# Cross-attention on one core: an output bias on one partition, context rows loaded a round later, and two sets of context squares put behind fetches in SyncE's queue

## The chip, the cores and the metric

The kernel runs on one core of a Trainium2 chip. A core has five engines that run side by side: TensorE (PE, matrix multiplication), VectorE (DVE), ScalarE (ACT), GpSimd (POOL) and SyncE (SP). Here nearly every DMA is issued by SyncE, whose instructions run strictly in order. The metric is the device time of one launch in microseconds, the median of several runs.

## The reference

Sixty-four independent items b, each with text rows x[b] (256 x 512) and context rows c[b] (256 x 384), all in float32:

```
Q = layer_norm(x @ W_text + b_text) * g1 + beta1       # 256 x 512
V = c @ W_audio + b_audio
K = layer_norm(V) * g2 + beta2                         # 256 x 512
alpha = softmax(Q @ K.T / sqrt(512))                   # 256 x 256
out = layer_norm((alpha @ V) @ W_out + b_out + x) * g_out + beta_out
```

## The kernel before

Everything is tiled to 128 partitions: an item has two row tiles of x and two of c. The value path is folded: since the rows of alpha sum to one, (alpha @ V) @ W_out is (alpha @ c) @ (W_audio @ W_out) plus a row vector b_audio @ W_out + b_out. The folded weights are built once (`fold_multiply`, tile `wao`). The row vector is built in two steps: `bias_parts` sums, over four groups of rows, W_out's rows scaled by b_audio into `part` (128 x 512), and `fold_bias` multiplies `part` by a matrix of ones, which sums over the partitions and puts the same row on each of the 128 partitions; VectorE then adds `bo_sb`, the output bias broadcast to all partitions by a 256 KB DMA, while it takes the sum out of the accumulator (`bao`).

The matrix multiplications need operands with the contracted dimension on partitions. The kernel gets such transposes by way of DMA. `squares` issues four DMAs (lines 84 to 88) that lay a matrix out in blocks of 32 x 32, one DMA for each group of 32 partitions, and VectorE transposes within the blocks. For the inputs this is `load_c` (tile `cq`, 4 x 96 KB) and `load_x` (tile `xq`, 4 x 128 KB). For computed Q and K rows it is a round trip through device memory: `store` writes the normalised rows (`qr`, `kr`; 512 KB) to a scratch tensor (`qd`, `kd`) in one DMA, `fetch` reads it back as squares (`qq`, `kq`; 4 x 128 KB), `turn` transposes them into `qT` or `kT`, and `affine` lets ScalarE apply the scale and the shift. The exponentials take the same way (`ed`, `eq`). A fetch waits on SyncE until the store has landed, and all that is written behind it in the program waits too.

The schedule is written out by hand: each engine's instructions run in the order of the program. A prologue does the projections of items 0 and 1 and the foldings; then a loop of 62 rounds runs. Round b computes the scores and the softmax of item b, the query and key projections of item b + 2, the context product (`Attention.context`, L587) of item b - 1 and its output product, and finishes item b - 2. The squares of item b + 4 are loaded in round b. Plain rows are loaded too: `load_x_rows` for the residual and `load_c_rows` for the context product, each of which has three buffers. In round b the row loads are those of x[b] and of c[b + 1]. Both come in SyncE's order behind the squares and the fetch of the exponentials. The accumulators of the projections are six banks of pool `p_pj`.

The end of the prologue is where the change lies. In the program's order SyncE has there: store of k[0], the five small loads of the column vectors, fetch of k[0], store of q[0], `load_c(2)`, fetch of q[0], `load_x(2)`, store of k[1], the broadcast of the output bias, `load_c(3)`, fetch of k[1], `load_x(3)`, store of q[1], fetch of q[1]. Behind this begins round 0, and round 1 begins with the scores of item 1, which need `qT` and `kT` of item 1.

Of the kernel before, what the change touches and what calls it, by code (L numbers as in the profile page):

```python
# [9 lines left out]
F32 = mybir.dt.float32  # L10
AF = mybir.ActivationFunctionType
ALU = mybir.AluOpType
# [3 lines left out]
P = 128  # L16
# [6 lines left out]
def kernel(  # L23
# [41 lines left out]
    nc = tc.nc  # L65
# [3 lines left out]
    H = w_text.shape[1]  # L69
# [4 lines left out]
    const = ctx.enter_context(tc.tile_pool(name="const", bufs=1))  # L74
# [9 lines left out]
    def squares(dst, src):  # L84

        v = src.rearrange("(b j) (q f) -> q j b f", j=SQ, q=NQ)
        for q in range(NQ):
            nc.sync.dma_start(dst[q * SQ : (q + 1) * SQ], v[q])  # L88
# [7 lines left out]
    def load_c(b):  # L96
        cq = blk.tile([P, S // SQ, DA // NQ], F32, tag="cq", name=f"cq_{b}")
        squares(cq, c[b])
        blocks[b] = [cq]

    def load_x(b):
        xq = blk.tile([P, L // SQ, D // NQ], F32, tag="xq", name=f"xq_{b}")
        squares(xq, x[b])
        blocks[b].append(xq)
# [5 lines left out]
    def load_x_rows(b):  # L110
        x_rows[b] = xin.tile([P, LT, D], F32, tag="x", name=f"x_{b}")
        nc.sync.dma_start(x_rows[b], x[b].rearrange("(t p) d -> p t d", p=P))

    def load_c_rows(b):
        c_rows[b] = cin.tile([P, ST, DA], F32, tag="c", name=f"c_{b}")
        nc.sync.dma_start(c_rows[b], c[b].rearrange("(t p) d -> p t d", p=P))
# [16 lines left out]
    def row(v, name):  # L133
        t = const.tile([P, H], F32, tag=name, name=name)
        nc.sync.dma_start(t, v.rearrange("(o h) -> o h", o=1).broadcast_to([P, H]))
        return t
# [8 lines left out]
    x_rows, c_rows = {0: x_0}, {0: c_0}  # L145
# [21 lines left out]
    load_x(1)  # L167
    columns = const.tile([P, 5, HC], F32, tag="columns", name="columns")

    def load_vectors():  # L170
        for n, v in enumerate((g1, beta1, g2, beta2, b_audio)):
            nc.sync.dma_start(
                vectors[n * HC : (n + 1) * HC].rearrange("k (q i) -> k q i", q=NQ),
                v.rearrange("(q k i) -> k q i", q=NQ, i=SQ),
            )
# [21 lines left out]
    class RowTurn:  # L197


        def __init__(self, rows_sb, chunks, name):  # L200
            self.rows, self.chunks = rows_sb, chunks
            tag = "yr" if chunks == DC else "kT"
            self.ar = work.tile([P, 2, chunks, P], F32, tag=tag, name=f"{name}r")
            self.T = work.tile([P, chunks, 2 * P], F32, tag=name, name=f"{name}_0")
# [25 lines left out]
    def bias_parts():  # L230

        part = work.tile([P, D], F32, tag="e", name="part")
        nc.vector.tensor_scalar(part, wo_sb[:, 0, :], bac_sb[:, 0:1], None, ALU.mult)
        for k in range(1, HC):
            nc.vector.scalar_tensor_tensor(
                part, wo_sb[:, k, :], bac_sb[:, k : k + 1], part, ALU.mult, ALU.add
            )
        return part

    wao_sb = const.tile([P, AC, D], F32, tag="wao", name="wao")  # L240
# [17 lines left out]
    def fold_bias(part):  # L258

        ps = p_pj.tile([P, D], F32, tag="pj", name="ps_bao")  # L260
        nc.tensor.matmul(ps, lhsT=ones, rhs=part, start=True, stop=True)
        bao = const.tile([P, D], F32, tag="bao", name="bao")
        nc.vector.tensor_tensor(bao, ps, bo_sb, ALU.add)
        return bao

    def moments(mv, src, t):
# [242 lines left out]
    class Attention:  # L509
        def __init__(self, b):  # L510
            self.b, self.qT, self.kT = b, q.pop(b).T, k.pop(b).T
            self.c_sb, self.summed = c_rows[b], ()

        def scores(self, end=False):
            if end:
# [62 lines left out]
        def context(self):  # L578

            self.zT = work.tile([P, AC, L], F32, tag="zT", name="zT")  # L580
            self.ps_z = []
            for lo in range(0, AC, 2):
                n = min(2, AC - lo)
                ps = p_at.tile([P, 2, L], F32, tag="at", name="ps_z")
                for j in range(n):
                    for s in range(ST):
                        nc.tensor.matmul(  # L587
                            ps[:, j, :],
                            lhsT=self.c_sb[:, s, bass.ts(lo + j, P)],
                            rhs=self.eT[:, s, :],  # L590
                            start=(s == 0),
                            stop=(s == ST - 1),
                        )
                nc.scalar.copy(self.zT[:, lo : lo + n, :], ps[:, :n, :])
# [163 lines left out]
    def turn_next(b):  # L758
        xT[b] = turn_x(b)
        xs[b] = sum_x(xT.pop(b))  # L760
        cT[b] = turn_c(b)
        cs[b] = sum_c(cT.pop(b))
# [7 lines left out]
    q, k, xT, cT = {}, {}, {}, {}  # L770
# [41 lines left out]
    k[0].normalise()  # L812
    k[0].store()
    load_vectors()
    k[0].fetch()
    q[0].evict(0)
# [3 lines left out]
    centre(bt_row, mean_bt, 1)  # L820
    q[0].normalise()
    q[0].store()
    load_c(2)
    q[0].fetch()
    load_x(2)
    xT[1] = turn_x(1)
    k[1].products(6)
# [16 lines left out]
        nc.vector.tensor_scalar(v, v, scale, None, ALU.mult)  # L844
    k[1].normalise()
    k[1].store()
    bo_sb = row(b_out, "bo")
    load_c(3)
    k[1].fetch()
    load_x(3)  # L850
    fold_evict(0)
    fold_evict(1)
    k[0].turn()
    k[0].affine(g2_sb, be2_sb)
    part = bias_parts()
    q[1] = Blocks("q", 1, xs.pop(1), wt_blocks, bt_sb)
    q[1].products(1, 2, 6, 5)
# [15 lines left out]
    fold_multiply(2)  # L873
    fold_evict(2)
    bao_sb = fold_bias(part)
    wao_blocks = weights_of_three(wao_sb, "waosum")
    q[1].normalise()
# [4 lines left out]
    for b in range(B - 2):  # L882
        three = b + 3 < B
        at = Attention(b)
        at.scores()
        if done:
            done.o.leave(3, 4)
            done.o.leave(7)
            done.add_x()
        if three and b:  # L890
            turn_next(b + 3)
        if last:
            last.turn_e()
        at.maxima()
        at.exponentials()
        if not b:
            k[1].turn()
        q2 = q[b + 2] = Blocks("q", b + 2, xs.pop(b + 2), wt_blocks, bt_sb)
        q2.products(*((1, 6) if b else (1, 2, 6)))
        q2.leave(1)  # L900
        q2.leave(6)
        at.reciprocals()
        at.divide_e()
        if not b:
            k[1].affine(g2_sb, be2_sb)
        if b:
            q[b + 1].fetch()
            k[b + 1].fetch()
        at.store_e()
        if b + 4 < B:  # L910
            load_c(b + 4)
        if not b:
            at.fetch_e()
        if b + 4 < B:
            load_x(b + 4)
        if b:
            at.fetch_e()
            load_x_rows(b)
        if not three:
            load_x_rows(b + 1)  # L920
        load_c_rows(b + 1)
        if b == 1:
            go_sb = row(g_out, "go")
            beo_sb = row(beta_out, "beo")
        if done:
            done.statistics()
        q2.products(*((2, 5) if b else (5,)))
        q2.leave(2, 5)
        q2.products(3, 4)
        q2.leave(3, 4)  # L930
        q2.products(7)
        q2.leave(7)
        q2.square()
        q2.scales()
        q[b + 1].turn()
        if not b:
            turn_next(3)
        if done:
            done.shift(0)
            done.shift(1)  # L940
        if last:
            last.context()
        q[b + 1].affine(g1_sb, be1_sb)
        if b:
            k[b + 1].turn()
            k[b + 1].affine(g2_sb, be2_sb)
        if done:
            done.settle(0)
            done.settle(1)
            done.store()  # L950
        q2.normalise()
        q2.store()
        if last:
            last.start_products()
        k2 = k[b + 2] = Blocks("k", b + 2, cs.pop(b + 2), wa_blocks, ba_sb)
        k2.products(1, 6)
        k2.leave(1)
        k2.leave(6)
        k2.products(2, 5)
        k2.leave(2, 5)  # L960
        k2.products(3, 4)
        k2.leave(3, 4)
        k2.products(7)
        k2.leave(7)
        k2.square()
        k2.scales()
        k2.normalise()
        k2.store()
        if last:
            last.o.products(1, 6)  # L970
            last.o.leave(1)
            last.o.leave(6)
            last.o.products(2, 5)
            last.o.leave(2, 5)
            last.o.products(3, 4)
            last.o.products(7)
        done, last = last, at
# [112 lines left out]
```

## Time and profile before

| what | value |
|---|---|
| median of 3 runs | 1416.42 us (1416.02 to 1416.92) |
| the profiled execution | 1416.99 us, span 1415.2 us |
| PE busy | 1404.5 us, 99% |
| DVE busy | 1229.0 us, 87% |
| ACT busy | 935.1 us, 66% |
| POOL busy | 870.6 us, 62% |
| DMA | 322.58 MB, mean 228 GB/s |
| mean granted PE clock | 0.999 |

Times inside the profile are counted from the start of the span. The span is the profiled execution without what lies around it (1.8 us). "SPq" is SyncE's queue: its rows show how long the issue of a DMA took, and a separate view gives the time from issue to landing. PE and PEld are the matrix multiplications and the loads of their stationary operands. L numbers are lines of the kernel.

### The profile page before, as it was taken

The page shows a single profiled execution, that of the slowest core. Times are in us where ns is not written, and L with a number is a line of the kernel's source. Part 1 is how long each engine was busy: PE and PEld are TensorE (multiplying, and loading weights), DVE is VectorE, ACT ScalarE, POOL GpSimd, SP SyncE. Part 2 cuts the span into 40 slices and gives each one's busy share as a digit, 9 for nine tenths or more (in the row PEclk, how much of TensorE's full clock was granted, in tenths as well). Part 3 has the DMA queues.
Part 4 walks back from the last instruction along what each step waited for, and adds up shares of the span by engine and source line. Part 5 has one row for each costly group of instructions (what it writes and reads, how often), then busy time and mean ns, then how long its engine had stood idle before and what let it go on. Part 6 is the DMA issues. An engine that isn't in the chain of part 4 may idle for free.

```text
span 1415.2 us, 22762 instructions
## 1 busy us (share of the span) xinstructions
PE 1404.5 (99%) x6437; PEld 1219.7 (86%) x6437; DVE 1229.0 (87%) x1757; ACT 935.1 (66%) x2298; POOL 870.6 (62%) x1294
## 2 busy tenths in 40 slices
PE   9999999999999999999999999999999999999998
PEld 5788888888888888888888888888888888888885
DVE  5789888988988988988889889889888898898887
ACT  4667676676676676766766766767667667667663
POOL 5557656656666666566566666665665665666645
PEclk9999999999999999999999999999999999999999
DMA  7898887887888787887887887877888788788864
GB/s 198 212 249 245 243 238 220 240 241 221 234 232 229 232 228 236 234 226 237 229 233 232 220 241 233 227 238 228 226 242 239 221 236 239 222 235 226 229 199 125
DMA packets 450579, 322.58 MB, mean 228 GB/s; under 512 B 154900, under 2 KB 382996, under 8 KB 450452
## 3 DMA queue, kind: packets, MB, share of 16 engines
q1 hardware_dynamic: 450356, 320.98, 80.0%
q8 instruction: 52, 0.85, 0.3%
q14 instruction: 75, 0.61, 0.1%
q10 hardware_dynamic: 96, 0.13, 0.0%
HBM read 204.09 MB, written 116.92 MB: 227 GB/s over the span
## 4 chain that ended last, share of the span: by engine, by line
PE 94%; DMA 3%; DVE 1%; POOL 1%; SPq 1%; ACT 0%; issue 0%; DVEq 0%; ACTq 0%
PE ps_q L482 26%; PE ps_k L482 20%; PE ps_y L482 20%; PE ps_sc L521 15%; PE ps_z L587 12%; DMA qd<-qr 1%; PE ps_y L634 1%; DMA ba<-in_L_xattn_b_audio_dram 1%; DMA qq<-qd 0%; DMA xq<-in_x_dram 0%; DMA bt<-in_L_xattn_b_text_dram 0%; SPq L88 0%; DMA c<-in_ctx_dram 0%; DVE qr L494 0%; DMA kd<-kr 0%
## 5 line engine op out<-in xcount | busy, mean ns | idle before, releaser
L494 DVE TENSOR_TENSOR qr<-ps_q,qr 128x512 f32<-128x512 f32 x252 | 174.3, 692 | 88.3 <-PE ps_q L482 85.3
L521 PE MATMUL ps_sc<-kT,qT 128*128 128x256 f32 x1024 | 231.7, 379 | 1.1 <-ACT qT L453 1.1
L348 POOL TENSOR_SCALAR ve<-var 128x2 f32<-128x2 f32 x126 | 43.1, 342 | 290.3 <-ACT junk L387 290.1
L521 PEld LDWEIGHTS ps_sc<-kT,qT 128*128 128x128 f32 x1024 | 194.2, 190 | 28.8 <-ACT qT L453 2.1
L538 ACT ACTIVATE e<-ps_sc,nmx 128x256 f32<-128x256 f32 x128 | 59.4, 469 | 228.7 <-DVE nmx L531 228.7
L603 POOL TENSOR_TENSOR yr<-yr,x 128x512 f32<-128x512 f32 x124 | 155.6, 1277 | 70.2 <-DVE yr L494 70.2
L482 PE MATMUL ps_q<-wtsum,xsum 128*128 128x256 f32 x756 | 193.8, 379 | 0.2 <-POOL xsum L312 0.2
L494 DVE TENSOR_TENSOR kr<-ps_k,kr 128x512 f32<-128x512 f32 x252 | 174.3, 692 | 22.1 <-DVE kr L494 0.5
L494 DVE TENSOR_TENSOR yr<-ps_y,yr 128x512 f32<-128x512 f32 x248 | 171.5, 692 | 21.8 <-DVE yr L494 0.5
L482 PE MATMUL ps_k<-wa,cT 128*128 128x256 f32 x630 | 177.1, 379 | 0.0
L587 PE MATMUL ps_z<-eT,c 128*128 128x256 f32 x768 | 176.2, 379 | 0.0
L482 PE MATMUL ps_y<-wao,zT 128*128 128x256 f32 x620 | 174.1, 379 | 0.0
L350 POOL TENSOR_TENSOR rstd<-ve,nhalf 128x2 f32<-128x2 f32 x192 | 157.1, 818 | 16.0
L587 PEld LDWEIGHTS ps_z<-eT,c 128*128 128x128 f32 x768 | 145.9, 190 | 20.3 <-issue 0.5
L482 PEld LDWEIGHTS ps_q<-wtsum,xsum 128*128 128x128 f32 x756 | 143.6, 190 | 20.0 <-POOL xsum L312 0.6
L453 ACT ACTIVATE qT<-qT,columns 128x256 f32<-128x256 f32 x256 | 132.9, 591 | 8.0 <-DVE qT L91 8.0
L482 PEld LDWEIGHTS ps_k<-wa,cT 128*128 128x128 f32 x630 | 119.6, 190 | 16.2
L453 ACT ACTIVATE kT<-kT,columns 128x256 f32<-128x256 f32 x256 | 132.0, 586 | 1.4 <-DVE kT L446 1.0
L415 ACT ACTIVATE kr<-kr,rstd 128x512 f32<-128x512 f32 x126 | 84.0, 714 | 72.3 <-POOL rstd L350 72.3
L482 PEld LDWEIGHTS ps_y<-wao,zT 128*128 128x128 f32 x620 | 117.7, 190 | 16.0
L387 ACT ACTIVATE junk<-kr 128x512 f32<-128x512 f32 x126 | 79.4, 630 | 77.5 <-DVE kr L494 73.1
L482 PE MATMUL ps_q<-wt,xT 128*128 128x256 f32 x504 | 129.1, 379 | 0.0
(159 smaller groups left out, 2973.0 us busy)
## 6 DMA issues: line engine op xcount, KB each, us to landing
kd<-kr SPq DMA_DIRECT2D x64, 512.0 KB, 3.1
kq<-kd SPq DMA_DIRECT2D x256, 128.0 KB, 3.4
qd<-qr SPq DMA_DIRECT2D x64, 512.0 KB, 4.8
qq<-qd SPq DMA_DIRECT2D x256, 128.0 KB, 3.3
xq<-in_x_dram SPq DMA_DIRECT2D x252, 128.0 KB, 2.8
x<-in_x_dram SPq DMA_DIRECT2D x63, 512.0 KB, 4.2
out_dram<-yr SPq DMA_DIRECT2D x62, 512.0 KB, 4.8
cq<-in_ctx_dram SPq DMA_DIRECT2D x252, 96.0 KB, 2.4
```

Source lines behind the costliest of these rows:

```text
L348: nc.gpsimd.tensor_scalar(ve, var, EPS, None, ALU.add)
L350: nc.gpsimd.tensor_tensor(r, ve, nhalf[:, :n], ALU.pow)
L387: nc.scalar.activation(junk, self.rows[:, t, :], AF.Square, scale=1.0 / math.sqrt(H), accum_out=self.var[:, t : t + 1],)
L415: nc.scalar.mul(row, row, self.r[t])
L453: nc.scalar.activation(self.T[:, k, :], self.T[:, k, :], AF.Identity, bias=bet[:, k : k + 1], scale=gam[:, k : k + 1],)
L482: nc.tensor.matmul(place, lhsT=side, rhs=w, start=(i == 0), stop=(i == len(pairs) - 1))
L494: add = lambda o, i0, i1: nc.vector.tensor_tensor(o, i0, i1, ALU.add)
L521: nc.tensor.matmul(self.sc[:, t, :], lhsT=self.qT[:, k, bass.ts(t, P)], rhs=self.kT[:, k, :], start=(k == 0), stop=(k == HC - 1),)
L538: nc.scalar.activation(self.e[:, t, :], self.sc[:, t, :], AF.Exp, bias=self.nmx[:, t : t + 1], accum_out=self.den[:, t : t + 1],)
L587: nc.tensor.matmul(ps[:, j, :], lhsT=self.c_sb[:, s, bass.ts(lo + j, P)], rhs=self.eT[:, s, :], start=(s == 0), stop=(s == ST - 1),)
L603: nc.gpsimd.tensor_tensor(self.y[:, t, :], self.y[:, t, :], x_rows[self.b][:, t, :], ALU.add)
L634: nc.tensor.matmul(ps, lhsT=self.zT[:, k, bass.ts(t, P)], rhs=wao_sb[:, k, :], start=(k == 0), stop=(k == AC - 1),)
```

## The change

The output bias is now loaded onto one partition (2 KB), as the first of the small loads in `load_vectors`, and VectorE adds it to partition 0 of `part` before the multiplication by ones, which then distributes it; the eviction into `bao` is a plain copy. From round 1 on, round b loads the context rows of item b instead of b + 1; round 0 loads none, and the last round of the loop, number 61, loads those of items 61 and 62. `Attention` looks its context rows up when it uses them. In the prologue the fetch of q[0] comes ahead of `load_c(2)`, and the fetch of k[1] ahead of `load_c(3)`.

```
+    bo_sb = const.tile([1, H], F32, tag="bo", name="bo")
     def load_vectors():
+        nc.sync.dma_start(bo_sb, b_out.rearrange("(o h) -> o h", o=1))
         for n, v in enumerate((g1, beta1, g2, beta2, b_audio)):
...
     def bias_parts():
...
+        nc.vector.tensor_tensor(part[:1], part[:1], bo_sb, ALU.add)
         return part
...
     def fold_bias(part):
...
-        nc.vector.tensor_tensor(bao, ps, bo_sb, ALU.add)
+        nc.vector.tensor_copy(bao, ps)
...
     class Attention:
         def __init__(self, b):
-            self.c_sb, self.summed = c_rows[b], ()
+            self.summed = ()
...
         def context(self):
-                            lhsT=self.c_sb[:, s, bass.ts(lo + j, P)],
+                            lhsT=c_rows[self.b][:, s, bass.ts(lo + j, P)],
...
     q[0].store()
+    q[0].fetch()
     load_c(2)
-    q[0].fetch()
     load_x(2)
...
     k[1].store()
-    bo_sb = row(b_out, "bo")
+    k[1].fetch()
     load_c(3)
-    k[1].fetch()
     load_x(3)
...
         if b:
             at.fetch_e()
             load_x_rows(b)
+            load_c_rows(b)
         if not three:
             load_x_rows(b + 1)
-        load_c_rows(b + 1)
+            load_c_rows(b + 1)
```

More of the change, by code (lines that the diff above doesn't have):

```diff
@@ L168 @@
     columns = const.tile([P, 5, HC], F32, tag="columns", name="columns")
+    bo_sb = const.tile([1, H], F32, tag="bo", name="bo")
     def load_vectors():
+        nc.sync.dma_start(bo_sb, b_out.rearrange("(o h) -> o h", o=1))
         for n, v in enumerate((g1, beta1, g2, beta2, b_audio)):
@@ L237, in bias_parts @@
             )
+        nc.vector.tensor_tensor(part[:1], part[:1], bo_sb, ALU.add)
         return part
@@ L262, in fold_bias @@
         bao = const.tile([P, D], F32, tag="bao", name="bao")
-        nc.vector.tensor_tensor(bao, ps, bo_sb, ALU.add)
+        nc.vector.tensor_copy(bao, ps)
         return bao
@@ L511, in __init__ @@
             self.b, self.qT, self.kT = b, q.pop(b).T, k.pop(b).T
-            self.c_sb, self.summed = c_rows[b], ()
+            self.summed = ()
         def scores(self, end=False):
@@ L588, in context @@
                             ps[:, j, :],
-                            lhsT=self.c_sb[:, s, bass.ts(lo + j, P)],
+                            lhsT=c_rows[self.b][:, s, bass.ts(lo + j, P)],
                             rhs=self.eT[:, s, :],
@@ L822 @@
     q[0].store()
+    q[0].fetch()
     load_c(2)
-    q[0].fetch()
     load_x(2)
@@ L846 @@
     k[1].store()
-    bo_sb = row(b_out, "bo")
+    k[1].fetch()
     load_c(3)
-    k[1].fetch()
     load_x(3)
@@ L918 @@
             load_x_rows(b)
+            load_c_rows(b)
         if not three:
             load_x_rows(b + 1)
-        load_c_rows(b + 1)
+            load_c_rows(b + 1)
         if b == 1:
```

## The prediction

> **What bounds the kernel now.** I read the chain that ended last first, since it names the engine that sets the end.
>
> ```profile
> PE 94%; DMA 3%; DVE 1%; POOL 1%; SPq 1%; ACT 0%; issue 0%; DVEq 0%; ACTq 0%
> ```
>
> TensorE (PE) carries the span. So a change can only act by making or closing a gap in PE's work, and the next view is everything that PE ever waited for. It has five rows, 3.6 us in all; this is the only one that lies beside the changed lines.
>
> ```profile
> PE ps_sc L521 <- ACT qT L453: 1.1, 1, 1.1
> ```
>
> It is the scores of round 1, and in the timeline of PE every later matmul of the main loop follows without idle time: a round is 21.58 us of matmuls (60.17 to 81.75 and on). Whatever delays or hastens that one instruction at 60.17 us moves the whole rest, one for one. The chain in order of time, cut to the first 66 us, tells what it waits for: the second queries' rows are stored (`qd<-qr`), fetched back as squares (`qq<-qd`), transposed, scaled, multiplied.
>
> ```profile
> 31.59 4.86 DMA qd<-qr
> ...
> 37.85 3.42 DMA qq<-qd
> ...
> 49.58 3.60 DMA qd<-qr
> ...
> 54.59 3.52 DMA qq<-qd
> ...
> 59.52 0.61 ACT qT L453
> 60.17 3.90 PE ps_sc L521 x16
> ```
>
> All these transfers are issued by one in-order queue, SyncE's (SP), so its timeline is the view that the change is read in. Columns: start, time, line, transfer, count.
>
> ```profile
> 31.59 0.40 SPq L425 DMA_DIRECT2D qd<-qr  x1
> 32.04 3.20 SPq L88 DMA_DIRECT2D cq<-in_ctx_dram  x4
> 36.51 1.79 SPq L88 DMA_DIRECT2D qq<-qd  x4
> 38.35 1.96 SPq L88 DMA_DIRECT2D xq<-in_x_dram  x4
> 40.42 0.39 SPq L425 DMA_DIRECT2D kd<-kr  x1
> 40.85 0.47 SPq L135 DMA_DIRECT2D bo<-in_L_xattn_b_out_dram  x1
> 41.36 2.62 SPq L88 DMA_DIRECT2D cq<-in_ctx_dram  x4
> 44.78 1.79 SPq L88 DMA_DIRECT2D kq<-kd  x4
> 46.63 1.92 SPq L88 DMA_DIRECT2D xq<-in_x_dram  x4
> 49.58 0.38 SPq L425 DMA_DIRECT2D qd<-qr  x1
> ```
>
> A fetch cannot be issued before its store has landed. Now each store is followed by work that fills that wait: context 2's squares (32.04 to 35.24) in the wait for `qd`, and the bias and context 3's squares (40.85 to 43.98) in the wait for `kd`. SP stands still for only 1.27 us (35.24 to 36.51) and 0.80 us (43.98 to 44.78). The store of q[1] at 49.58 starts when its rows are ready (ScalarE's `qr` ends at 49.56); SP had been free since 48.55.
>
> **The change in SP's queue.** It takes the fillers out of the two waits and puts them behind the fetches, in front of the next store.
>
> First wait. The store of q[0] stays at 31.59: the bias row's new issue (one, about 0.4 us by its neighbours, the loads of `vectors`) goes where SP sat from 29.26 to 29.71 waiting for k[0]'s store, so it costs 0 to 0.1 us. Does q[0]'s store land sooner without four transfers behind it? Three rows say that a store's landing depends on what is ahead: `kd` at 26.83 with an idle queue ahead took 2.81 us; `kd` at 40.42, straight behind four x squares, took 4.3; and the median `kd`, which has fetches right behind it, takes 3.1. Here the four `kq` fetches (29.71 to 31.50) are still ahead. I keep 4.86 us, hence the fetch at 36.51 as before; the low end is 3.6 (`qd` at 49.58), which gives 1.26 us back.
>
> Then SP issues `qq` until 38.30, `cq` of context 2 (four issues; 1.93 us, as the four x squares behind a fetch take 1.92 to 1.96; the high end is 3.20, the row of the same tile directly behind a store) until 40.3, and `xq` until 42.3. So k[1]'s store, whose rows are ready at 37.85, goes out at 42.3 instead of 40.42: 1.9 us late.
>
> Second wait. Straight behind x squares the landing is 4.3 us as now (low end 2.8): 46.6. Fetch `kq` 46.65 to 48.45, `cq` of context 3 to 50.4, `xq` to 52.4. The bias broadcast's 0.47 us is gone, but it lay in the wait and saves nothing there. The store of q[1] therefore goes out at 52.45 instead of 49.58, now bound by SP and not by its rows. Before, SP had been free for 1.0 us ahead of it and it landed in 3.60; now it follows the x squares directly, so I take 4.3: landed at 56.75 instead of 53.18. That is 3.55 us late; fetch, transpose and scaling keep their times, so PE's scores start at 63.7 instead of 60.17 and PE's gap grows from 1.1 to 4.6 us. **Sum of this part: +3.5 us.**
>
> The sum of issue times is not the only way to see this: from the start of `qq` at 36.51 to the landing of `kd` is 8.2 us now, with `qq`, `xq` and `kd` to move; four squares of context 2 between them add their 1.9 us, 10.1 us; the same pattern follows once more from `kq`. 36.45 + 2 x 10.1 gives 56.65. Both ways agree within 0.1 us.
>
> **What else it touches, costed at nothing.** PE's work between 44 and 59 us: any slip there is swallowed by the 4.6 us gap, as long as it is smaller. x squares of 2 now land near 45.4 (last issue 41.8 + 3.6) and the transpose that needs them starts at 46.24: 0.8 us left. `kq` of k[1] lands 1.9 us later, so VectorE's transpose at 49.91 goes to 51.8, and the five evictions of q[2] queued behind it end near 56.9 instead of 55.06; the accumulators that PE needs again from 57 us are the first ones emptied, by 54.4, and VectorE is free before the transpose of q[1], its next job, at 61.8. ScalarE's `e` and its store likewise stand before that.
>
> The bias: one 2 KB load and one VectorE add on one partition, queued between `part` (ends 39.28) and the transpose of q[0] at 41.39, in 2.12 us of idle time. Its nearest rows are 444 ns (L233) and 752 ns (L235); it fits, and would cost up to 0.75 us only if `qq` landed over a microsecond sooner. The eviction at L263 (0.65 us) becomes a copy of the same size; its reader is a round away.
>
> Context rows a round later: one issue and 384 KB leave round 0, and every round b then loads context b where it loaded b + 1. In the round at 643 us the load goes out at 658.03, and the next round's context matmuls, which now read it, start at 674.3: 16.3 us against a median landing of 4.8. Only the last main round issues one row load more (about 0.45 us at 1367.8), in front of SP's 2.8 us of idle time before 1371.53; its reader starts at 1380.49, so 7.9 us are left after a landing of 4.8. If either cover were gone, the shortfall would go straight to PE.
>
> **A gap of 4.6 us and PE's clock.** At the end of the trace PE's last matmul ends at 1408.35 and the windows show the granted clock (the third column from the right) holding for 4.1 us and then halved:
>
> ```profile
> 1408.40:1412.50 4.10, 0.00 (x0) 0.00 (x0) 3.83 (x9) 0.00 (x0) 2.12 (x3) 1.00 0.33 123
> 1412.60:1415.20 2.60, 0.00 (x0) 0.00 (x0) 0.00 (x0) 0.00 (x0) 0.00 (x0) 0.50 0.51 177
> ```
>
> So idle time of 4.2 us did bring it down, and 4.6 us may or may not. Its price is bounded by the cold start: there the first 12 matmuls of L195 took 2.93 us, where the same shape at L224 goes 6 in 0.82; that and the stretch behind it lost about 1.4 to 2.6 us. I take nothing for the likeliest case and keep 2.6 for the range.
>
> [...]
>
> **The rivals.** (1) The clock falls in the gap: +3.5 plus 1.4 to 2.6, 1421.3 to 1422.5. For it: the end of this trace; against: a gap barely longer than the time it held. (2) The landings are shorter: with fewer transfers in flight the three stores land in about 4.2, 3.8 and 3.8 us, and 0.7 + 0.5 + 0.5 come off: about +1.8, 1418.2. For it: q[1]'s own 3.60; against: the 4.3 behind x squares. (3) Not slower at all: stores land as on an idle queue. With 3.6, 2.8 and 2.8 us the sum is 3.55 - 1.26 - 1.5 - 1.5 = -0.7, PE's gap falls to 0.4, and at most the whole 1.1 us of waiting can go: 1415.3 to 1416.4. It decides where the three landings together are below 9.9 us (13.46 in my sum). Against it: x squares are directly ahead of two of the three stores.
>
> **How the numbers follow.** The profiled execution took 1416.99 us (its span of 1415.2 and 1.8 around it); with 3.5 that is 1420.5. The median of the runs, 1416.42, is 0.57 lower: 1419.9. What a measurement can tell from no change is about 0.2%, 2.8 us, that is 1419.25. The forecast (+2.3 to +4.6, the upper end from slower issues of the context squares) has 0.62, of which 0.5 lies over the bound and 0.12 under it; rival 1 has 0.20, rival 2 0.12, rival 3 0.06. Slower: 0.5 + 0.2 = 0.70; same: 0.12 + 0.12 + 0.04 = 0.28; faster 0.02, for a cause that I do not see, since PE has only 3.6 us of waits to give back. The range leaves out rival 3, part of rival 2, and what exceeds rival 1: 1417.6 to 1423.0.
>
> **What would show it.** In the profile after: the wait of `ps_sc` L521 for `qT` near 4.6 us instead of 1.1; SP waiting over 4 us for `qd` and for `kd` where it now waits 1.3 and 0.8; k[1]'s store near 42.3 and q[1]'s near 52.4 with no wait for `qr`; no PE wait at L587 for context rows; the rounds still 21.58 us. Wrong if q[0]'s store lands before 35.5, if q[1]'s store still waits for its rows, if a granted clock of 0.5 stands in the windows after 60 us, or if PE waits for `c`.

## The result and the profile after

The changed kernel is slower by 0.17%: ratio 1.0017, 95% interval 1.0011 to 1.0023; medians 1418.31 us against 1415.9 us, 22 runs each. The difference of 2.4 us lies in the predicted range, clear of no change, and inside the 0.2% below which the prediction counted a change as none. The profiled execution took 1417.74 us, its span is 1416.0.

The split of the chain that ended last is unchanged; TensorE (PE) still carries it:

```profile
PE 94%; DMA 3%; SPq 1%; DVE 1%; POOL 1%; issue 0%; ACT 0%; DVEq 0%; ACTq 0%; POOLq 0%
```

What PE waited for in the whole span (engine, line, what for: us in total, times, longest). The wait before round 1's scores has grown from 1.1 us, and among the five rows there is none at L592, the context product that reads the rows loaded later:

```profile
PE ps_sc L526 <- ACT qT L458: 3.0, 1, 3.0
```

SyncE's queue in the same stretch as before (start, us, line, transfer):

```profile
30.55 0.40 SPq L430 DMA_DIRECT2D qd<-qr  x1
35.59 1.82 SPq L88 DMA_DIRECT2D qq<-qd  x4
37.45 1.93 SPq L88 DMA_DIRECT2D cq<-in_ctx_dram  x4
39.42 1.93 SPq L88 DMA_DIRECT2D xq<-in_x_dram  x4
41.46 0.39 SPq L430 DMA_DIRECT2D kd<-kr  x1
45.14 1.79 SPq L88 DMA_DIRECT2D kq<-kd  x4
46.98 1.93 SPq L88 DMA_DIRECT2D cq<-in_ctx_dram  x4
48.97 1.92 SPq L88 DMA_DIRECT2D xq<-in_x_dram  x4
51.38 0.38 SPq L430 DMA_DIRECT2D qd<-qr  x1
54.86 1.79 SPq L88 DMA_DIRECT2D qq<-qd  x4
```

This execution runs about 1.04 us ahead at the store of q[0] (30.55 against 31.59), so rows are to be read as distances from it. Then SyncE (SP) stands still in both waits, which its own waits say:

```profile
SPq L88 <- DMA qd<-qr: 4.6, 1, 4.6
SPq L88 <- DMA kd<-kr: 3.2, 1, 3.2
```

Before, the same two rows were 1.2 and 0.7 us, and there was one of 0.9 us, in which the store of q[1] waited for its rows (`qr`). That one is gone: the rows are ready at 48.42 us, 3 us ahead of the store, which is now late by the queue. The chain of the same stretch:

```profile
30.55 5.02 DMA qd<-qr
...
41.46 3.66 DMA kd<-kr
...
50.95 0.42 issue
51.38 3.41 DMA qd<-qr
...
56.20 2.63 DMA qq<-qd
...
60.89 3.91 PE ps_sc L526 x16
```

From the store of q[0] to that of q[1] it is 20.83 us, where it was 17.99: 2.84 us more. From there to the scores it is 9.51 us, where it was 10.59: 1.08 us less. The difference of the two, 1.8 us, is about what PE's wait has grown by.

### The profile page after: what moved, and what is told of

Its sections match the earlier page's. It is cut to its first block, busy times and chain, and to the rows that moved or that the text cites. A ratio compares the mean times of both kernels' runs of the same rounds, so it can differ in the third digit from the quotient of the medians.

```text
span 1416.0 us, 22763 instructions
## 1 busy us (share of the span) xinstructions
PE 1403.7 (99%) x6437; PEld 1219.5 (86%) x6437; DVE 1230.8 (87%) x1758; ACT 937.5 (66%) x2298; POOL 871.7 (62%) x1294
## 4 chain that ended last, share of the span: by engine, by line
PE 94%; DMA 3%; SPq 1%; DVE 1%; POOL 1%; issue 0%; ACT 0%; DVEq 0%; ACTq 0%; POOLq 0%
PE ps_q L487 26%; PE ps_k L487 20%; PE ps_y L487 20%; PE ps_sc L526 15%; PE ps_z L592 12%; SPq L88 1%; DMA qd<-qr 1%; PE ps_y L639 1%; DMA wo<-in_L_xattn_W_out_dram 1%; DMA kd<-kr 0%; DMA x<-in_x_dram 0%; DMA wt<-in_L_xattn_W_text_dram 0%; DMA c<-in_ctx_dram 0%; DVE yr L499 0%; DMA qq<-qd 0%
## 5 line engine op out<-in xcount | busy, mean ns | idle before, releaser
L592 PE MATMUL ps_z<-eT,c 128*128 128x256 f32 x768 | 176.2, 379 | 0.0
L592 PEld LDWEIGHTS ps_z<-eT,c 128*128 128x128 f32 x768 | 145.9, 190 | 20.3 <-issue 0.5
```

The costliest lines, as they stand in the source:

```text
L592: nc.tensor.matmul(ps[:, j, :], lhsT=c_rows[self.b][:, s, bass.ts(lo + j, P)], rhs=self.eT[:, s, :], start=(s == 0), stop=(s == ST - 1),)
```

## The experiments

Ratios are against the kernel before on the same chip, with their 95% intervals.

### The order alone, and the rest alone

With both fetches put back into the changed kernel:

```
     q[0].store()
-    q[0].fetch()
     load_c(2)
+    q[0].fetch()
...
     k[1].store()
-    k[1].fetch()
     load_c(3)
+    k[1].fetch()
```

> The changed kernel with both fetches put back behind the context squares; the bias on one partition and the later context rows stay. If the order in SyncE's queue is the whole cost: TensorE's wait for qT at the scores of round 1 goes back from 3.0 us to 1.1 or less, ratio 0.9993 to 1.0004. Rival, the context rows or the bias cost something: the ratio stays near 1.0017. Beside it, the landing of k[1]'s store, which here has context squares but no bias broadcast behind it: 4.3 us if only what is ahead of a store in the queue counts, about 3.7 if the broadcast behind it had slowed it.

Ratio 0.9994 (0.9985 to 1.0003), median 1414.94 against 1415.6 us. PE's wait for `qT` at the scores of round 1 is gone altogether. Part of that is not the order: the fetch of q[0] could go out 3.4 us after its store here, against 4.9 in the kernel before, and the last section has what goes with that. k[1]'s store landed in 3.9 us, between the two values expected.

The opposite, the kernel before with nothing but the two fetches moved:

```
     q[0].store()
+    q[0].fetch()
     load_c(2)
-    q[0].fetch()
...
     k[1].store()
     bo_sb = row(b_out, "bo")
+    k[1].fetch()
     load_c(3)
-    k[1].fetch()
```

> The kernel before with nothing but the two fetches moved ahead of the context squares (the bias broadcast stays, between k[1]'s store and its fetch). If the order is the whole cost: ratio 1.0012 to 1.0022, TensorE's wait for qT near 3 us. Rival, the cost comes from the other two edits: ratio near 1.0000 and a wait near 1.1 us.

Ratio 1.0022 (1.0014 to 1.0031), PE's wait 3.1 us; here the store of q[0] landed in 4.53 us, much as before. So the order is the cost. k[1]'s store landed in 3.63 us with the 256 KB broadcast directly behind it, as fast as in the three profiles of the changed kernel (3.63 to 3.79), which has no broadcast there: no slowing by it is seen.

The two other edits, each alone on the kernel before. The bias (`Attention` looks its context rows up as in the changed kernel, which gives the same rows):

```
+    bo_sb = const.tile([1, H], F32, tag="bo", name="bo")
...
+        nc.sync.dma_start(bo_sb, b_out.rearrange("(o h) -> o h", o=1))
...
+        nc.vector.tensor_tensor(part[:1], part[:1], bo_sb, ALU.add)
...
-        nc.vector.tensor_tensor(bao, ps, bo_sb, ALU.add)
+        nc.vector.tensor_copy(bao, ps)
...
-    bo_sb = row(b_out, "bo")
```

> The kernel before with only the bias edit: 2 KB on one partition instead of the 256 KB broadcast. If it is hidden: ratio 0.9993 to 1.0003; k[1]'s store, with no broadcast behind it, lands in 3.6 to 4.0 us instead of 4.3, and TensorE's wait for qT is 0 to 1.1 us. Rival, the VectorE add or the extra issue costs something: a ratio above 1.0005.

Ratio 0.9997 (0.9988 to 1.0005): hidden, as far as a time can say, since here too q[0]'s fetch could go out 3.4 us after its store and PE had no wait for `qT`, which may cover a cost of up to 1 us. k[1]'s store landed in 4.0 us, the upper end of what was expected. The context rows:

```
-            self.c_sb, self.summed = c_rows[b], ()
+            self.summed = ()
...
-                            lhsT=self.c_sb[:, s, bass.ts(lo + j, P)],
+                            lhsT=c_rows[self.b][:, s, bass.ts(lo + j, P)],
...
         if b:
             at.fetch_e()
             load_x_rows(b)
+            load_c_rows(b)
         if not three:
             load_x_rows(b + 1)
-        load_c_rows(b + 1)
+            load_c_rows(b + 1)
```

> The kernel before with only the context rows a round later. If it is hidden: ratio 0.9995 to 1.0004, no wait of TensorE for context rows at the context product, rounds of 21.58 us, TensorE's wait for qT 1.1 us as before. Rival, the shorter lead costs something in every round: 62 rounds with 0.05 us each would be 3 us, ratio 1.002.

Ratio 1.0001 (0.9993 to 1.0010): hidden too, PE's wait for `qT` 1.2 us and none at the context product.

### One fetch at a time

The changed kernel with only q[0]'s fetch moved:

```
     k[1].store()
-    k[1].fetch()
     load_c(3)
+    k[1].fetch()
```

> The changed kernel with only the fetch of q[0] moved; k[1]'s is put back behind the squares of context 3. By the queue's own account k[1]'s store goes out 1 us late, but the store of q[1] had 1.0 us of room in front of it, so most of that is absorbed: TensorE's wait 1.1 to 1.6 us, ratio 1.0000 to 1.0005. Rival, each fetch costs its half: ratio 1.0008, wait 2.0 us.

Ratio 1.0008 (0.9999 to 1.0017), PE's wait 1.7 us: a little more than the queue's account gave. The ratio is the rival's, the wait lies between the two, and the interval holds both, so this run does not decide between them. With only k[1]'s fetch moved:

```
     q[0].store()
-    q[0].fetch()
     load_c(2)
+    q[0].fetch()
```

> The changed kernel with only the fetch of k[1] moved; q[0]'s is put back behind the squares of context 2. By the queue's account the wait for k[1]'s store is bare (about 3.7 us), the squares of context 3 come behind the fetch, and q[1]'s store goes out 0.5 to 0.9 us after its rows are ready: TensorE's wait 1.6 to 2.1 us, ratio 1.0003 to 1.0008. Rival, each fetch costs its half: ratio 1.0008, wait 2.0 us; the sum of this and the other half then equals 1.0017, where the queue's account says that the two alone make less than both together.

Ratio 1.0006 (0.9997 to 1.0015), PE's wait 2.4 us, more than expected. Whether the two alone make less than both together, as the account said, cannot be told: 0.08% and 0.06% add up to 0.14%, and the intervals reach across the 0.17% of both.

### More issues in front of the next store

Four unused loads of squares behind the context squares, at both places (`again` is 128 x 8 x 64, 256 KB each time):

```
+    def load_again(b):
+        squares(again, c[b][:, : 64 * NQ])
...
     q[0].fetch()
     load_c(2)
+    load_again(2)
     load_x(2)
...
     k[1].fetch()
     load_c(3)
+    load_again(3)
     load_x(3)
```

> The changed kernel with four more loads of squares (64 KB each, not used) behind the context squares at both places, so that each next store has 1.93 us more of issues in front of it. If the issue time in front of the stores is the cost: both stores go 1.97 us later each, TensorE's wait for qT is 3.0 + 3.9 = 6.9 us, the clock falls in every run, since that is twice the 3.4 us, and the ratio is 1.0050 to 1.0065; 1.0040 to 1.0047 if the clock plays no part. Rival, the cost is not in issue time: under 1 us more, ratio below 1.0025.

Ratio 1.0054 (1.0042 to 1.0066), from five runs. The issue times are as expected: from the fetch of q[0] to the store of k[1] 7.95 us (changed kernel 5.87), from the fetch of k[1] to the store of q[1] 8.10 us (6.24), 3.9 us more together. PE's wait in the profiled execution was only 4.0 us, because there PE itself came to the gap 1.1 us later and the store of q[0] landed in 3.22 us instead of 5.02. The windows of PE tell the rest (stretch, length, busy time of PE, PEld, DVE, ACT and POOL, granted clock, DMA share, GB/s):

```profile
57.99:61.40 3.41, 1.09 (x6) 0.61 (x4) 0.24 (x1) 0.00 (x0) 0.00 (x0) 1.00 0.85 242
61.40:64.81 3.41, 1.71 (x4) 1.45 (x5) 3.41 (x4) 2.37 (x5) 1.05 (x2) 0.50 0.77 182
64.81:68.23 3.42, 3.42 (x9) 2.70 (x9) 3.07 (x6) 1.78 (x5) 3.34 (x7) 0.50 0.95 297
68.23:71.60 3.37, 3.37 (x17) 2.96 (x17) 3.37 (x5) 2.24 (x5) 2.92 (x6) 1.00 0.02 8
```

The clock halves at 61.40 us, 2.3 us into the idle time, which lasts from 59.09 to 63.10. It is still halved after a stretch of 3.41 us of which PE was busy for half, and is back after the next, in which PE was busy throughout: 6.8 us at half clock. (With the order alone and with only k[1]'s fetch moved it came back after 2.94 and 3.08 us of 3.41.)

### Has the clock a share?

The changed kernel was run twice more, each time beside a version that fills a part of PE's idle time at the end of round 0 (the result of the filler is not used):

```
+        if not b:
+            keep_busy(6)
         done, last = last, at
```

> The changed kernel itself once more, beside the three that follow. Ratio 1.0011 to 1.0023, single runs between 1416.4 and 1421.5 us; where a single run is over 1420 its mean granted clock should be 0.996 and not 0.998, since the idle time of about 3 us then brought TensorE's clock down.

> The changed kernel with six matrix multiplications of ones by ones in TensorE's idle time at the end of round 0 (about 1.4 us; the result is not used). If part of the cost is that the clock falls in the idle time of some runs: the late start of the scores stays, but no run lies above 1419.5 us, the mean clock is 0.997 or 0.998 everywhere, and the ratio is 1.0010 to 1.0015. Rival, the clock plays no part: the spread and the ratio stay as without the filler.

The changed kernel: 1.0018 (1.0010 to 1.0027), 1418.88 us. With the filler, 1.50 us long: 1.0011 (1.0003 to 1.0020), 1417.74 us, one run of twelve at 1419.73 where the expectation had a limit of 1419.5. Without the filler five of twelve runs lie above that. In a single run the mean clock is no sign of a fall: the half clock at the end takes 2.6 us of the span in the profile before and 4.9 in the profile after, a difference of 2.3 us, where a fall lasted 3.41. Over many runs it is. Of the 45 runs of the changed kernel (22 of the result and the 23 of this section) 18 have a mean clock under 0.998: six at 0.996, all above 1420 us with a median of 1420.3, and twelve at 0.997 with a median of 1419.0; the 21 at 0.998 have 1418.3 and the six at 0.999 have 1417.2. Of the 23 runs with a filler none is under 0.998. Then the longer filler, ten multiplications instead of six:

> The changed kernel again, as the reference for the longer filler beside it: ratio 1.0014 to 1.0023. Its profile may or may not show the clock at 0.5 for 3.4 us behind the idle time; it did in one of the two so far.

> The changed kernel with ten multiplications of ones by ones (about 2.4 us, result not used) in TensorE's idle time. [...] If the clock has a share in the cost: its median lies 0.7 to 1.5 us under the changed kernel's in this call, ratio 1.0009 to 1.0014, as with the short filler, and no clock of 0.5 behind the idle time. Rival, all of the cost is the idle time itself and the short filler's 1.1 us were chance: no difference from the changed kernel, or up to 0.3 us more where the filler runs into the scores.

The changed kernel: 1.0020 (1.0011 to 1.0029), 1418.4 us. With 2.39 us of filler: 1.0012 (1.0003 to 1.0021), 1417.05 us, and its eleven runs lie between 1416.55 and 1417.8. So in both comparisons the filled version is 1.1 to 1.4 us faster than the changed kernel beside it (95% intervals from drawing the single runs anew: 0.1 to 2.5 and 0.8 to 1.7 us), and its spread is smaller. Its scores start about as late: at 61.12 us with the short filler and 60.45 with the long one, against 61.97 and 60.07 in the changed kernel's two profiles, but they take 3.90 us with either filler and 5.47 and 5.41 without. Here PE doing useless work cost less than PE standing still. The rows behind it are the windows of the changed kernel in the first of the two comparisons:

```profile
59.37:62.79 3.42, 0.82 (x4) 0.59 (x4) 2.76 (x3) 1.48 (x3) 0.24 (x1) 1.00 0.74 188
62.79:66.20 3.41, 3.41 (x10) 2.62 (x9) 3.12 (x5) 1.84 (x5) 3.25 (x6) 0.50 0.82 225
```

and PE's timeline there, whose scores take 5.47 us instead of 3.91:

```profile
61.97 5.47 PE L526 MATMUL ps_sc<-kT,qT 128*128 128x256 f32 x16 [3.42 <-ACT qT L458]
```

In the changed kernel of the second comparison the same is seen from 60.3 us on; the profiled execution that the result above was read from happens to show no fall, nor do the two with filler.

### The squares behind the next store

The changed kernel with the squares of 3 moved past the store of q[1]:

```
     k[1].store()
     k[1].fetch()
-    load_c(3)
-    load_x(3)
...
     q[1].store()
+    load_c(3)
     q[1].fetch()
+    load_x(3)
```

> The changed kernel with the squares of context 3 issued behind q[1]'s store, in the wait for it, and the squares of x 3 behind q[1]'s fetch. If the cost is what stands in front of the next store: q[1]'s store goes out when its rows are ready, near 49 us, it lands in about 3 us since nothing is ahead of it, the fetch follows at once, TensorE's wait is under 1 us, ratio 0.9992 to 1.0000. Rival, a fetch ahead of its squares is what costs: ratio 1.0010 or more; or the squares of 3 come too late for round 0 and the wait moves to VectorE's transposes of them, 0.5 us or more of waiting for xq near 62 us.

Ratio 0.9999 (0.9991 to 1.0008). The store goes out at 48.98 and lands in 2.98 us, as expected, and the loss is gone. PE's wait is 1.9 us all the same and not under 1: the fetch issued at 52.04 now comes behind the context squares (49.40 to 51.85), and VectorE gets `qq` only at 58.46, 6.4 us after that issue, where it was 4.1 us in the profile after (54.86 to 58.95). The rival's second half is seen too: VectorE waits 0.9 us for the x squares, twice.

```profile
58.46 1.25 DVE L91 STREAM_TRANSPOSE qT<-qq 128x1024 f32<-128x1024 f32 x1 [3.19 <-DMA qq<-qd]
60.61 1.25 DVE L91 STREAM_TRANSPOSE xT<-xq 128x1024 f32<-128x1024 f32 x1 [0.91 <-DMA xq<-in_x_dram]
```

The lowest ratio of all is that of the changed kernel with the fetches put back, 0.9994; its interval includes no change.

## Why the prediction was right, and where it was wrong

**The mechanism and the place were right.** The two waits of SP lost their cover, the store of q[1] became bound by the queue, and the scores of round 1 came late; the order alone gives 1.0022 and its removal takes the loss away. The issue of the context squares took 1.93 us as assumed. From the store of q[0] to that of q[1] the sum had 20.86 us, and the profile shows 20.83. That it agrees so closely is luck: q[0]'s store took 0.16 us more than assumed, k[1]'s 0.64 less, a pause of 0.42 us was not foreseen, and the two other profiles of the changed kernel show 20.41 and 20.28. The second way of adding it up was no check, since it used the same landings. One slip changed nothing: the round that begins at 60.17 us lasts 22.03 us by the chain, and the 21.58 us hold from the next one on.

**The bias, the context rows and the last round cost nothing**, as costed: 0.9997 and 1.0001 alone. In the profile after, the add on one partition took 0.68 us and ended at 39.2, a microsecond ahead of the transpose that it stands in front of, and PE waits for nothing from 75 us on.

**The step that was mis-sized is the last hop, from q[1]'s store to the scores.** I let the store land in 4.3 us because x squares were directly ahead of it, and left the fetch at its 3.52 us. In the three profiles of the changed kernel the store landed in 3.41, 3.78 and 3.57 us and the fetch, from its last issue, in 2.63, 2.90 and 2.65. So of the 3.55 us in the sum PE's gap kept 1.8 to 2.3: from 1.1 to 2.96, 3.42 and 2.91 us. In this the prediction's rival 2 (1418.2 us) came nearer than its forecast (1419.9): it had landings of 4.2, 3.8 and 3.8 us, and the three profiles show 4.4 to 5.0, 3.6 to 3.8 and 3.4 to 3.8. The fetch's gain goes with a transfer that is not the kernel's: in the profile before, a 16 KB transfer of the instruction queue lies in the time of this fetch, which took 4.9 us from its first issue,

```profile
q8 instruction: 1, 0.02, 1.9%
```

(DMA queues from 54.6 to 58.1 us: packets, MB, share), and in the profile after, where the fetch took 4.0 us, it lies between 51.4 and 54.8, in the store's time. In the other runs whose chain shows the fetch it took 4.7 to 5.3 us in four (only q[0]'s fetch moved, only k[1]'s, the long filler, the rows alone) and 4.0 to 4.2 in five; where such a transfer lies in those was not shown. That the later store has moved the fetch behind that transfer is so the author's estimate from two profiles, and the sum could not know it.

**The reading of landings was too simple.** That only what is ahead of a store counts rested on three rows. k[1]'s store, which had x squares ahead of it in every run, landed in 3.9 to 4.3 us in the five profiles where context squares were issued behind it, and in 3.3 to 3.8 us in eight of the nine where the queue waited for it (4.0 in the ninth, with the squares moved behind the next store). So by the means of these groups, 4.0 and 3.6 us, the covers cost the store about 0.4 us; taking them away gave that back, which the sum had at nothing. Against that SP waited 0.42 us more in front of q[1]'s store, the "issue" row of the chain. What it waited for is not shown; with four more loads at both places a pause of 0.44 us stands between two of these loads, at 49.75 us, and none in front of the store.

**The clock's share was put at nothing and is not.** The sum took no fall for the likeliest case because at the end of the trace the clock held for 4.1 us after the last matmul. The fillers put its share at 1.1 to 1.4 us of the 2.8 to 2.9 us that the changed kernel lost beside them, so two errors, one of about 1.5 us too much and one of 1.2 too little, partly cancelled, and that the total came so near is in part luck. A granted clock of 0.5 after 60 us, which the prediction named as a sign of being wrong, stands in two of the three profiles of the changed kernel. Two more of its signs missed: SP's wait for `kd` was 3.2 us and not over 4, and PE's wait was 2.9 to 3.4 us and not 4.6.

The end of the trace was one case, and the runs show others. In the kernel before, the clock was halved 4.2 us after PE's last matmul (1408.35 to 1412.59); at the end of the profile after it was 2.0 us (1409.08 to 1411.11), and with four more loads 2.3. Beside the gap, PE had been busy in the 3.41 us ahead of the fall for 0.50 us (the changed kernel in the second comparison), 0.77 (the order alone), 0.82 and 1.09, as shown above, and 1.38 (only k[1]'s fetch moved, where PE's whole wait was 2.4 us). With the short filler the clock stayed at 1.00 through a stretch of 3.42 us with 3.37 us of work and one of 3.41 with 1.70, and in the profile after through these two:

```profile
56.02:59.43 3.41, 1.91 (x9) 1.33 (x7) 0.47 (x1) 0.15 (x2) 0.93 (x2) 1.00 0.86 246
59.43:62.85 3.42, 1.96 (x8) 1.34 (x9) 3.39 (x5) 2.62 (x6) 1.30 (x2) 1.00 0.79 198
```

What makes the clock fall was not shown. The length of the idle time does not tell these cases apart, since it fell with 2.4 and 2.9 us and held with 2.96; the work in the stretches does, but where the stretches begin in the two that held is the author's choice, and no run varied it alone. One fall costs up to 1.7 us by estimate, half of 3.41; the scores that met one in the changed kernel took 5.47 us instead of 3.91, 1.56 more. The 3.4 us that the expectation for four more loads counts with is shown by no run as a bound for idle time: the clock fell with idle times of 2.4 to 4.0 us, and 3.41 us is how long it stayed halved.

**The chances.** 0.70 stood on slower by over 0.2%; the ratio came out at 0.17%, its interval across the bound. With the gap's growth of about 2 us and a fall of the clock in some executions, the outcome had to lie close to that bound.

## What to carry to other kernels

Between a store to device memory and the fetch that needs it, an in-order queue had three to five microseconds to fill here; transfers that nobody waits for belong there, and putting them behind the fetch charges their issue time to the next store in the chain. A change in the prologue's queue is paid once and shows in one row, the wait of the bounding engine, so look for that row before summing. Idle times of TensorE of 2.4 to 4.0 us here went with a halved clock in five profiles of six, and 1.50 or 2.39 us of useless multiplications in them made the kernel 1.1 to 1.4 us faster.

## What was not expected of the hardware

- With idle times of 3.4, 3.1, 2.9 and 2.4 us TensorE's clock was halved for 3.41 us, and with one of 4.0 us for 6.8 us. With one of 2.96 us (the profile after) it was not, nor with three of 1.7 to 1.9 us.
- A 16 KB load of instructions, on a queue of its own, goes with a later landing of q[0]'s store. That store landed in 4.4 to 5.0 us in nine profiles and in 3.2 to 3.5 us in five, with and without context squares behind it. In four of the nine, the kernel before and the three of the changed kernel, the queues show such a load between 30 and 34 us; in the five they show none from 31.1 to 34 us, most of the store's time. For q[1]'s store nothing of the kind is seen: with such a load in its time it landed in 3.41 us in the profile after, without one in 3.60 in the kernel before. Here are the queues from 31.6 to 36.4 us in the kernel before:

```profile
q1 hardware_dynamic: 1964, 1.22, 88.7%
q8 instruction: 1, 0.02, 2.1%
```

Why the load is not there in five of the kernels was not found; these are the ones with the fetches put back, with the bias alone, with only q[0]'s fetch moved, with four more loads and with the long filler. In the first two the early landing can explain why PE had no wait at all: q[0]'s fetch could go out 3.4 us after its store, 1.5 us sooner than in the kernel before, whose wait was 1.1 us. So by estimate the ratios of these five may hold up to about a microsecond, 0.08%, that is neither the order's nor the bias's. In the kernel before and with the order alone that store landed in 4.86 and 4.53 us, so by estimate their 1.0022 holds at most 0.3 us of it.
